# Nine value projections of the first attention quarter, moved ahead of their periods

## The chip, the core and the metric

The kernel runs on one core of a Trainium2 chip, as one program. The time is the device time of one execution in microseconds, the median of several runs. The engines are TensorE (PE, with its weight loads as PEld), VectorE (DVE), ScalarE (ACT) and GpSimd (POOL); SyncE (SP) issues nearly all DMAs of the part that is looked at here.

## What is computed

Two transformer layers, each an attention and a mixture of experts with residuals, on 16 batches of 128 tokens with 512 channels. Only layer 0's attention is touched. It has a self-attention and a cross-attention to a context, 16 query heads and 8 key/value heads each, and one projection over the outputs of both. Cut to what matters, the cross-attention does this:

```python
q  = layernorm_per_head(fp8_linear(ln(x), wqx))        # 16 heads of 128
k  = layernorm_per_head(ctx @ w_kv_x[:1024].T)         # 8 heads
v  = ctx @ w_kv_x[1024:].T                             # 8 heads, only a projection
p  = softmax(q @ k.T / sqrt(128))
out_x = p @ v                                          # then quantized and projected
x  = x + fp8_linear(concat(out_self, out_x), wproj)
```

The value of a batch depends on the context and on the value weights alone, on nothing of x. The matrix products are in float32 or, where one side is exact in fewer bits, in a weight split in two parts.

## The kernel before

Class `Layer0` works through four quarters (`QUARTERS`): cross-attention heads 0 to 7, cross-attention heads 8 to 15, then the two halves of the self-attention. In each quarter it goes over the 16 batches. Batch b of quarter q has the number n = 16q + b. The change touches quarter 0, batches 0 to 9.

The work on a batch is cut into named steps, and these are software-pipelined by hand. `ORDER` is a list of (step, lag): in period p, each step in the list is emitted in turn for batch n = p - lag. All engines follow this order strictly (`InOrder` keeps the program order), so an instruction that waits holds up everything behind it on its engine. SP also issues its DMAs in the order in which they are emitted.

The steps that matter here, with their lag:

- `ln1` to `lnn2` (0): two layernorms of x on DVE, with the power on POOL. `trX` (1): PE transposes the result. `lnT` (1): ACT scales it. `zmul`, `zclip`, `zmsk`, `zadd`, `zsub` (1): POOL, DVE, POOL, DVE bring it onto the quantization grid; the result is `xq`, the queries' input.
- `Kp`, `sqK`, `rsK`, `kn`, `trK`, `kT` (1, kT 2): key projection (PE), squares (ACT), rsqrt (POOL), scaling (DVE), transpose (PE), affine (ACT).
- `Vp`, `v` (3): value projection (PE) and its copy to the tile `v` (ACT); `load_v` fetches its input `xv` from `ctxT` one period earlier. The tag `v` has 3 buffers, `xv` has 2, and the PSUM tag `mm` has 3 banks.
- `Qp0`, `sqQ0`, `rsQ0`, `qn0`, `trQ0`, `qT0`, `sc0`, `nm0`, `exp0`, `pn0`, `trP0`, `pT0`, `pv0` and the same with 1: two chunks of four heads, from query projection to the product with `v` (`pv` uses it at lag 4).
- `po0`, `po1`, `xr`: the output projection and the residual.
- Steps beginning with `W` prepare weights ahead: DVE takes means and cuts a weight into a high and a low part, POOL centres and subtracts, ACT scales, casts and sums the low part.

Before the periods, `start` does the first batch's steps by hand and begins the first weights: the key weights (two pieces of 512 KB), four pieces of query weights (256 KB each), then `xv` and the two pieces of value weights. On PE, the order in the opening is: transpose of x, `Kp`, `Vp`, `trK`, `Qp0`.

In the profile, most instructions have line 69, that of the helper that records them; they are told apart by tile names. `mm<-w,xv` is a value projection, `mm<-w,xk` a key projection, `tr<-ident,xn` is `trX`.

Of the kernel before, what the change touches and what calls it, by code (L numbers as in the profile page):

```python
# [11 lines left out]
F32 = mybir.dt.float32  # L12
# [11 lines left out]
P = 128  # L24
NB = 16
D = 512
# [56 lines left out]
class Ops:  # L83
# [34 lines left out]
    def t(self, pool, shape, dt, tag, bufs=None):  # L118
        self.uid += 1
        return pool.tile(shape, dt, name=f"{tag}_{self.uid}", tag=tag, bufs=bufs)  # L120
# [252 lines left out]

PIECE_STEPS = "lsmckhua"


# [31 lines left out]
def flat(a):  # L410
    return a.rearrange("p c t -> p (c t)")
# [6 lines left out]
class Layer0:  # L418
# [12 lines left out]
    def __init__(self, ops, tc, args, x_dram, vec, router, small, wpool, work, dram, banks, kept_pool, ahead):  # L431
        self.plain, self.tc = ops.nc, tc
        self.kept_pool, self.ahead = kept_pool, ahead
        ops.nc = Engines(tc, ops.nc)
        nc, t = ops.nc, ops.t
        self.ops, self.args, self.x_dram, self.vec, self.router = ops, args, x_dram, vec, router
        self.wpool, self.work, self.banks = wpool, work, banks

        self.kept = {
            kind: [t(dram, [P, D], F32, f"kept_{kind}{b}") for b in range(NB)]  # L440
            for kind in ("lnT", *KINDS)
        }
        self.rin = t(small, [P, 16], F32, "rin")
        nc.vector.reciprocal(self.rin, vec[:, V_INS : V_INS + 16])
        self.rsm = t(small, [P, 32], F32, "rsm")
        nc.vector.reciprocal(self.rsm, vec[:, V_SMOOTH : V_SMOOTH + 32])

        self.ws2 = t(small, [P, 4], F32, "ws2")
        nc.vector.scalar_tensor_tensor(
            self.ws2, vec[:, S_WQ : S_WQ + 4], 1.0 / P, vec[:, S_WQ : S_WQ + 4], ALU.mult, ALU.mult  # L450
        )
        self.pscale = t(small, [P, 1], F32, "pscale")
        nc.vector.tensor_tensor(
            self.pscale, vec[:, S_PROJ_W : S_PROJ_W + 1], vec[:, S_PROJ_IN : S_PROJ_IN + 1],
            ALU.mult,
        )

        self.lw = t(small, [P, 8], F32, "lw")
        for i, (col, scale, by) in enumerate((
            (QLN_W, S_WQ, SCALE), (QLN_B, None, SCALE), (KLN_W, S_WK, 1.0), (KLN_B, None, 1.0),  # L460
            (QXLN_W, S_WQX, SCALE), (QXLN_B, None, SCALE), (KXLN_W, None, 1.0),
            (KXLN_B, None, 1.0),
        )):
            s = 1.0 if scale is None else vec[:, scale : scale + 1]
            nc.vector.tensor_scalar(
                self.lw[:, i : i + 1], vec[:, col : col + 1], s, by, ALU.mult, ALU.mult
            )


        self.w = {}  # L470
        self.units = {"w": W_UNITS, **KEPT_UNITS}
        self.todo = [(q, what) for q in range(4) for what in WEIGHTS]
        self.pieces = [p for q, what in self.todo for p in self.pieces_of(q, what)]
        self.begun, self.finished, self.slots, self.low_steps = [], set(), {}, []
        self.dram, self.made, self.freed, self.period, self.at_step = dram, {}, [], 0, 0
        self.raws = [p for p in self.pieces if p[0] == 0 or p[1] != "v" or self.is_pair(*p[:2])]
        self.pieces = [p for p in self.pieces if p[0]]

        self.low, self.any_low, self.adds = {}, {}, {}
        self.at = [{} for _ in range(4 * NB)]  # L480
# [156 lines left out]

        return added

    def begin(self, centre=None):  # L640
        piece = self.raws.pop(0)
        self.begun.append((piece, self.prepare(*piece, centre)))
        self.advance(self.begun[-1], "l")

    def advance(self, job, until):

        piece, steps = job
        while steps and PIECE_STEPS.index(steps[0][0]) <= PIECE_STEPS.index(until):
            steps.pop(0)[1]()
# [157 lines left out]
    def load_v(self, n):  # L807
        ops, t, s = self.ops, self.ops.t, self.at[n]
        quarter, b = divmod(n, NB)
        if QUARTERS[quarter][0] == 1:  # L810
            s["xv"] = t(self.work, [P, NC, P], F32, "xv", 2)
            ops.nc.sync.dma_start(out=s["xv"], in_=self.args["ctxT"][b])
        else:
            s["xv"] = t(self.work, [P, NC, P], F32R, "xv", 2)
            self.fetch("v", b, s["xv"])
# [6 lines left out]

    def fetch(self, kind, b, out):
        self.ops.nc.sync.dma_start(out=flat(out).bitcast(F32), in_=self.kept[kind][b])

    def step(self, name, n):

        ops, nc, t, work = self.ops, self.ops.nc, self.ops.t, self.work  # L830
        if name[0] != "W":
            quarter, b = divmod(n, NB)
            half = QUARTERS[quarter][0]
            s = self.at[n]
        if name[0] == "W":
            self.piece_step(name, n)
            return
        if name in STEP_NAMES:
            if quarter == 3:
                if name == "rn1":  # L840
                    s["job"] = Routing(self.router, b, s["xr"], work, self.banks)
                getattr(s["job"], STEP_NAMES[name])()
            return
        if name[:2] == "ln" or name == "trX":
            if quarter == 0:
                self.norm_step(name, b, s)
            return
        if name[0] in "zw":
            i = "zw".index(name[0])
            if i < len(MADE[quarter]):  # L850
                self.made_step(name[1:], MADE[quarter][i], b, s)
            return
        c = name[-1]
        if c in "01":
            self.chunk_step(name[:-1], int(c), n, s)
        elif name == "Kp":
            s["k_ps"] = self.project(n, s["xk"], "k")
        elif name == "sqK":
            s["k_ss"] = self.squares(s["k_ps"])
        elif name == "rsK":  # L860
            s["k_rs"] = self.head_rsqrt(
                s["k_ss"], self.ws2[:, 1:2] if half == 0 else 1.0 / P
            )
        elif name == "kn":
            s["kn"] = self.head_scale(s["k_ps"], s["k_rs"], "kn")
        elif name == "trK":
            s["k_tr"] = ops.transpose4(self.banks, s["kn"])
        elif name == "kT":
            s["kT"] = self.affine(s["k_tr"], 2 if half == 0 else 6, "kT", 3)
        elif name == "Vp":  # L870
            s["v_ps"] = self.project(n, s["xv"], "v")
        elif name == "v":
            s["v"] = t(work, [P, D], F32, "v", 3)
            if half == 0:
                nc.scalar.activation(
                    s["v"], s["v_ps"], AF.Copy, scale=self.vec[:, S_WV : S_WV + 1]
                )
            else:
                nc.scalar.copy(s["v"], s["v_ps"])
        elif name == "xr":  # L880
            x = s["xr"]
            nc.vector.scalar_tensor_tensor(x, s["po"], self.pscale, x, ALU.mult, ALU.add)
            nc.sync.dma_start(out=self.x_dram[b], in_=x)
# [135 lines left out]
    def start(self):  # L1019

        nc = self.ops.nc
        self.load(0)
        for what in ("k", "q0"):
            for _ in self.pieces_of(0, what):
                self.begin(nc.vector if what == "q0" else None)
        keys, queries = self.begun[:2], self.begun[2:]
        self.load_v(0)
        for _ in self.pieces_of(0, "v"):
            self.begin()
        for name in ("ln1", "lnp1", "lnn1", "ln2", "lnp2", "lnn2", "trX", "lnT"):  # L1030
            self.step(name, 0)
        self.advance(keys[0], "c")
        for name in ("zmul", "zclip"):
            self.step(name, 0)
        self.advance(keys[1], "c")
        for job in queries:
            self.advance(job, "s")
        for name in ("zmsk", "zadd", "zsub", "Kp", "sqK"):
            self.step(name, 0)
        for job in queries[:2]:  # L1040
            self.advance(job, "u")
        for name in ("rsK", "Vp", "v", "kn", "trK", "kT"):
            self.step(name, 0)
        for job in queries[2:]:
            self.advance(job, "u")

# [6 lines left out]
    def run(self):  # L1053
# [4 lines left out]
        for period in range(4 * NB + lags["xr"]):  # L1058
            self.period = period
            for call, lag in (  # L1060
                (self.load, 0), (self.load_v, lags["Vp"] - 1), (self.load_x, lags["xr"] - 1),
            ):
                n = period - lag
# [4 lines left out]
            for at, (name, lag) in enumerate(ORDER):  # L1068
                if at % 4 == 0:
                    while self.freed and self.freed[0][0] <= period * len(ORDER) + at:  # L1070
                        _, tag, n = self.freed.pop(0)
                        self.units[tag] += n
                    self.refill()
                self.at_step = period * len(ORDER) + at
                if name[0] == "W":
                    lag -= lags["Wl" + name[2]] - 1
                n = period - lag
# [923 lines left out]
```

## Time and profile before

| | |
|---|---|
| median of 3 runs | 3702.06 us (3697.73 to 3706.18) |
| the profiled execution | 3698.0 us, span 3696.2 us |
| mean granted PE clock | 0.982 |
| PE busy | 3532.1 us (96% of the span) |
| DVE, ACT, POOL busy | 1756.6, 1500.5, 1265.6 us |
| quarter 0, to the end of period 12 | the first 264.9 us |
| DMA queue of SP | 338.49 MB, 27.3% of 16 engines' span |

Busy times overlap, since the engines work side by side. An engine can be less busy than PE over the whole span and still set the pace of a stage, so the profile is read by stretches. A timeline line gives the start, the time from the first to the last instruction of a merged group, the engine, the operation, the tiles and the shape; the bracket at its end is the idle time of the engine before it, and what ended that.

### The profile page before, as it was taken

The numbers are of one execution on the slowest core, as the hardware profiler recorded it, in microseconds if no ns is written. First come the engines' busy times: TensorE is split into PE (matmuls) and PEld (weight loads), VectorE is DVE, ScalarE is ACT, GpSimd is POOL, SyncE is SP. The second block draws the span as 40 slices with busy tenths as digits, with TensorE's granted clock in tenths as the row PEclk, the third lists the DMA queues.
The fourth block names the chain that finished last, engine by engine and source line by source line (L and its number), as shares of the span: only waits on it lengthen the run. The fifth ranks groups of instructions, "written<-read, shape, count | busy, mean of one in ns | idle before, by whom it ended". The sixth has DMA issues, their size and how long they took to land. (4 is left out here: it accounts for less than half of the span.)

```text
span 3696.2 us, 42676 instructions
## 1 busy us (share of the span) xinstructions
PE 3532.1 (96%) x13220; PEld 2111.1 (57%) x13220; DVE 1756.6 (48%) x4203; ACT 1500.5 (41%) x5601; POOL 1265.6 (34%) x1596
## 2 busy tenths in 40 slices
PE   6899999999999699999999999899999999997998
PEld 3666666788888444444444454455555555554655
DVE  6888899877688521100000000445555555553111
ACT  5777677788877111101100101443444343441111
POOL 6566677654244222101110100423333333321332
PEclk8999999999999799999999999999999999998999
DMA  4556755744523133453332331000001010006333
GB/s 159 167 175 205 260 199 194 275 147 145 177 90 122 52 115 98 135 167 100 105 91 63 104 76 25 31 23 30 27 22 35 22 32 19 21 12 236 69 63 55
DMA packets 156777, 382.80 MB, mean 104 GB/s; under 512 B 18080, under 2 KB 21312, under 8 KB 154752
## 3 DMA queue, kind: packets, MB, share of 16 engines
q1 hardware_dynamic: 138848, 338.49, 27.3%
q0 software_dynamic: 17696, 41.43, 5.9%
q8 instruction: 119, 1.95, 0.2%
q14 instruction: 114, 0.93, 0.1%
HBM read 266.32 MB, written 113.52 MB: 103 GB/s over the span
## 5 line engine op out<-in xcount | busy, mean ns | idle before, releaser
L69 PE MATMUL h<-xT,w 128*128 128x512 f32 x1024 | 467.2, 594 | 4.0 <-PEq L1322 1.1
L69 PE MATMUL o<-w,hT 128*128 128x512 f32 x1024 | 460.8, 592 | 0.0
L69 ACT ACTIVATE hT<-h 128x512 f32<-128x512 f32 x128 | 76.3, 596 | 852.8 <-PE h L69 852.8
L69 PEld LDWEIGHTS o<-w,hT 128*128 128x128 f32 x1024 | 194.2, 190 | 243.7 <-issue 243.0
L69 DVE COPY xT<-tr 128x512 f32<-128x512 f32 x79 | 54.4, 688 | 572.4 <-PE tr L69 572.4
L69 PEld LDWEIGHTS h<-xT,w 128*128 128x128 f32 x1024 | 189.6, 190 | 231.0 <-issue 229.3
L69 ACT ACTIVATE p<-sc,sm_nm 128x128 f32<-128x128 f32 (+1 forms) x768 | 302.7, 420 | 20.9 <-PE tr L69 10.4
L69 PE MATMUL mm<-w,xq 128*128 128x512 f32 x1024 | 275.8, 411 | 5.5 <-DVE xq L69 4.0
L69 PE MATMUL sc<-kT,qT 128*128 128x128 f32 (+1 forms) x1536 | 267.4, 310 | 4.7 <-ACT qT L69 4.4
L69 ACT ACTIVATE hn_sq<-mm 128x128 f32<-128x128 f32 x768 | 214.8, 280 | 128.1 <-PE mm L69 105.4
L69 POOL DMA_INDIRECT x_dram<-y,e_target x40 | 62.6, 1564 | 572.0 <-ACT y L69 562.3
L69 PE MATMUL pv<-pT,v 128*128 128x256 f32 (+1 forms) x768 | 255.8, 456 | 1.4 <-ACT pT L69 1.4
L69 PEld LDWEIGHTS sc<-kT,qT 128*128 128x128 f32 x1536 | 222.4, 191 | 46.0 <-issue 29.7
L69 PE MATMUL mm<-c_wq,hT 128*128 128x512 f32 x512 | 231.4, 595 | 0.7 <-DVE qn L69 0.7
L69 PE MATMUL po<-c_wo,oT 128*128 128x512 f32 x512 | 231.4, 595 | 0.0
L69 DVE TENSOR_REDUCE sm_nm<-sc 128x4 f32<-128x512 f32 (+1 forms) x256 | 175.5, 685 | 92.1 <-PE sc L69 92.0
L69 PE MATMUL po<-w,cq 128*128 128x512 f32 x512 | 192.4, 457 | 24.8 <-DVE cq L69 3.4
L69 POOL TENSOR_TENSOR hn_rs<-hn_rs,mhalf 128x4 f32<-128x4 f32 x192 | 205.2, 1069 | 16.0
L69 PEld LDWEIGHTS mm<-w,xq 128*128 128x128 f32 x1024 | 185.4, 191 | 43.6 <-DVE xq L69 4.8
L69 ACT ACTIVATE rms_sq<-mm 128x128 f32<-128x128 f32 x384 | 106.8, 278 | 251.5 <-PE mm L69 230.8
L69 PE MATMUL h<-e_w,xT 128*128 (+1 forms) x624 | 200.5, 465 | 4.3 <-DMA e_w<-in_f_w 3.5
L69 PE MATMUL mm<-w,xk 128*128 128x512 f32 x512 | 187.3, 508 | 0.9 <-POOL w L69 0.8
(248 smaller groups left out, 6388.6 us busy)
## 6 DMA issues: line engine op xcount, KB each, us to landing
w<-in_f_w SPq DMA_DIRECT2D x128, 512.0 KB, 3.7
kept_w<-st SPq DMA_DIRECT2D x66, 512.0 KB, 2.9
w<-kept_w SPq DMA_DIRECT2D x66, 512.0 KB, 5.6
x_dram<-xr SPq DMA_DIRECT2D x64, 256.0 KB, 2.0
xr<-x_dram SPq DMA_DIRECT2D x64, 256.0 KB, 2.8
e_w<-in_f_w SPq DMA_DIRECT2D x8, 1408.0 KB
xk<-in_ctxT SPq DMA_DIRECT2D x32, 256.0 KB, 3.8
xv<-in_ctxT SPq DMA_DIRECT2D x32, 256.0 KB, 3.0
```

Source lines behind the costliest of these rows:

```text
L69: return self.tc.keep_in_program_order(call(*args, **kwargs))
```

## The change

The value weights are the first weights to be loaded, ahead of the key weights. Value projections of batches 1 to 9 are made early: four in the opening (`VALUES_FIRST`), and five at named places of periods 2 and 3 (`VALUES_AT`). Each is copied by ACT to a `v` tile and stored in DRAM. In their own periods, `load_v` fetches the stored value in place of the context, and the steps `Vp` and `v` do nothing. Batch 0's value is projected first of all. The order on PE in the opening becomes: `Vp` of batch 0, value 1, transpose of x, value 2, `Kp`, value 3, value 4, `trK`, `Qp0`, value 5. In periods 2 and 3, a value is emitted ahead of the step that `VALUES_AT` names, and its copy and store five steps later (`later`).

```diff
+VALUES_FIRST = 4
+VALUES_AT = ((2, "trX"), (2, "sc0"), (3, "trX"), (3, "trP0"), (3, "trQ1"))
...
     def load_v(self, n):
         ops, t, s = self.ops, self.ops.t, self.at[n]
         quarter, b = divmod(n, NB)
+        if n in self.values:
+            s["v"] = t(self.work, [P, D], F32, "v", 3)
+            ops.nc.sync.dma_start(out=s["v"], in_=self.values[n])
+            return
...
+    def load_value(self):
+
+        n = len(self.values) + 1
+        self.load_v(n)
+        self.values[n] = self.ops.t(self.dram, [P, D], F32, f"value{n}")
+
+    def value(self):
+
+        n = max(self.values)
+        ps = self.project(n, self.at[n]["xv"], "v")
+        if n < VALUES_FIRST + len(VALUES_AT):
+            self.load_value()
+
+        def keep():
+            v = self.ops.t(self.work, [P, D], F32, "v", 3)
+            self.ops.nc.scalar.copy(v, ps)
+            self.ops.nc.sync.dma_start(out=self.values[n], in_=v)
+
+        return keep
...
+        elif n in self.values and name in ("Vp", "v"):
+            pass
...
         self.load(0)
+        for _ in self.pieces_of(0, "v"):
+            self.begin(what="v")
+        self.load_v(0)
+        self.load_value()
         for what in ("k", "q0"):
             for _ in self.pieces_of(0, what):
                 self.begin(nc.vector if what == "q0" else None)
         keys, queries = self.begun[:2], self.begun[2:]
-        self.load_v(0)
-        for _ in self.pieces_of(0, "v"):
-            self.begin()
-        for name in ("ln1", "lnp1", "lnn1", "ln2", "lnp2", "lnn2", "trX", "lnT"):
+        for name in ("Vp", "v"):
+            self.step(name, 0)
+        for name in ("ln1", "lnp1", "lnn1", "ln2", "lnp2", "lnn2"):
+            self.step(name, 0)
+        keep = self.value()
+        for name in ("trX", "lnT"):
             self.step(name, 0)
         self.advance(keys[0], "c")
         for name in ("zmul", "zclip"):
             self.step(name, 0)
+        keep()
+        keep = self.value()
         self.advance(keys[1], "c")
         for job in queries:
             self.advance(job, "s")
-        for name in ("zmsk", "zadd", "zsub", "Kp", "sqK"):
+        for name in ("zmsk", "zadd", "zsub"):
+            self.step(name, 0)
+        keep()
+        for name in ("Kp", "sqK"):
             self.step(name, 0)
         for job in queries[:2]:
             self.advance(job, "u")
-        for name in ("rsK", "Vp", "v", "kn", "trK", "kT"):
+        keep = self.value()
+        for name in ("rsK", "kn"):
             self.step(name, 0)
+        keep()
+        keep = self.value()
+        for name in ("trK", "kT"):
+            self.step(name, 0)
+        keep()
         for job in queries[2:]:
             self.advance(job, "u")
...
                 self.at_step = period * len(ORDER) + at
+                if self.later and self.later[0][0] <= self.at_step:
+                    self.later.pop(0)[1]()
+                if (period, name) in VALUES_AT:
+                    self.later.append((self.at_step + 5, self.value()))
```

More of the change, by code (lines that the diff above doesn't have):

```diff
@@ L473, in __init__ @@
         self.pieces = [p for q, what in self.todo for p in self.pieces_of(q, what)]
+        self.values, self.later = {}, []
         self.begun, self.finished, self.slots, self.low_steps = [], set(), {}, []
@@ L638, in find_low, with begin @@
         return added
-    def begin(self, centre=None):
-        piece = self.raws.pop(0)
+    def begin(self, centre=None, what=None):
+        piece = next(p for p in self.raws if what in (None, p[1]))
+        self.raws.remove(piece)
         self.begun.append((piece, self.prepare(*piece, centre)))
```

## The prediction

> **What bounds the kernel now.** I read the page first:
>
> ```profile
> PE 3532.1 (96%) x13220; PEld 2111.1 (57%) x13220; DVE 1756.6 (48%) x4203; ACT 1500.5 (41%) x5601; POOL 1265.6 (34%) x1596
> ```
>
> TensorE (PE) bounds the whole, but the change touches 265 us of it. So second I cut that stretch at PE's transposes of a batch's input (step trX of batch n opens period n+1; the cuts are its starts on PE's timeline). Columns: length, then busy time of PE, PEld, DVE, ACT, POOL, granted clock, DMA.
>
> ```profile
> 0.00:38.51 38.51, 16.48 (x32) 7.29 (x32) 25.43 (x61) 13.64 (x34) 18.93 (x36) 0.87 0.69 237
> 38.51:57.29 18.78, 11.81 (x36) 7.06 (x37) 12.22 (x25) 8.01 (x31) 13.43 (x15) 0.81 0.35 99
> 57.29:74.74 17.45, 14.06 (x64) 10.45 (x65) 10.11 (x21) 12.21 (x48) 12.23 (x14) 0.90 0.30 91
> 74.74:94.45 19.71, 18.58 (x89) 12.85 (x87) 13.45 (x33) 17.52 (x68) 12.59 (x14) 1.00 0.36 108
> 94.45:124.07 29.62, 21.59 (x92) 14.97 (x91) 17.02 (x37) 19.18 (x72) 13.94 (x16) 0.88 0.41 133
> 124.07:206.63 82.56, 77.45 (x355) 53.01 (x353) 77.44 (x149) 62.99 (x242) 52.85 (x61) 1.00 0.55 185
> 206.63:226.06 19.43, 19.13 (x89) 13.27 (x90) 18.07 (x38) 13.74 (x58) 11.84 (x14) 1.00 0.47 162
> 226.06:245.46 19.40, 19.10 (x91) 13.22 (x90) 17.28 (x37) 14.94 (x62) 11.23 (x13) 1.00 0.53 180
> 245.46:264.87 19.41, 19.11 (x91) 13.23 (x90) 15.32 (x34) 15.48 (x64) 11.21 (x13) 1.00 0.52 177
> ```
>
> The lines are the opening with period 1, then periods 2, 3, 4, 5, 6 to 9, 10, 11, 12. PE has room in the first three. But from period 6 to 10 VectorE (DVE) is as full as PE: it also prepares later weights there. Third, the waits of 144.82 to 226.06, DVE's and PE's:
>
> ```profile
> DVE xn L69 <- POOL ln_rs L69: 2.7, 4, 0.7
> PE tr L69 <- DVE xn L69: 3.6, 4, 1.0
> ```
>
> In four periods DVE waits only 0.7 us each, on its own layernorm chain; PE waits for DVE. There DVE sets the 20.6 us, not PE. Fourth, PE's timeline of the start:
>
> ```profile
> 10.67 1.12 PE L69 MATMUL tr<-ident,xn 128*128 128x128 f32 x4 [10.67 <-DVE xn L69]
> 12.59 6.81 PE L69 MATMUL mm<-w,xk 128*128 128x512 f32 x8 [0.80 <-POOL w L69]
> 19.23 3.60 PE L69 MATMUL mm<-w,xv 128*128 128x512 f32 x8
> 27.68 1.12 PE L69 MATMUL tr<-ident,kn 128*128 128x128 f32 x4 [4.85 <-DVE kn L69]
> 38.51 1.11 PE L69 MATMUL tr<-ident,xn 128*128 128x128 f32 x4 [4.30 <-DVE xn L69]
> 39.42 5.04 PE L69 MATMUL mm<-w,xk 128*128 128x512 f32 x8
> 46.79 1.16 PE L69 MATMUL sc<-kT,qT 128*128 128x128 f32 x8 [1.89 <-ACT qT L69]
> 52.32 3.60 PE L69 MATMUL mm<-w,xq 128*128 128x512 f32 x8 [3.43 <-DVE xq L69]
> 57.29 0.63 PE L69 MATMUL tr<-ident,xn 128*128 128x128 f32 x4 [1.37 <-DVE sm_rs L69]
> 68.27 0.66 PE L69 MATMUL tr<-ident,qn 128*128 128x128 f32 x4 [3.28 <-DVE qn L69]
> ```
>
> PE's gaps here are latencies of a chain that runs through DVE, GpSimd (POOL) and ScalarE (ACT). Fifth, SP's waits from 8 to 12 us:
>
> ```profile
> SPq L693 <- DMA w<-in_wkvx: 1.4, 1, 1.4
> SPq L693 <- DMA raw<-in_wqx: 0.3, 1, 0.3
> ```
>
> SP issues again at 10.30, when the second 512 KB weight piece has landed, and at 10.9, when the 256 KB transfer behind it has: at the start transfers land in order of issue, at nearly 400 GB/s.
>
> **What moves.** A value projection is eight matmul records, 3.43 us from start to the next work (81.36 to 84.79). Nine of them, 30.9 us, leave periods 4 to 12. Four go into the opening, one each before trX and sc0 of period 2, three into period 3 (before trX, trP0, trQ1). The nine ACT copies (0.59) move along. Nine 256 KB stores are new; loading a kept value replaces loading ctxT. The built program has the same number of PE instructions and 18 more on SP.
>
> **Term 1, the opening.** PE runs in program order, and now two value projections (batches 0 and 1) stand ahead of the first transpose. They need both value pieces and xv. These take the places in SP's order that the key pieces and the first q piece had, and so the landing times: second piece 10.3, xv 10.9. PE starts at 11.0. Its price at the start: the first transposes took 1.12 against 0.60 later, so a cold projection costs 3.43 x 1.87 = 6.4; a warm one 3.4. I take 6.0 for the first, near the cold row since it follows 11 us of idleness, and 3.4 for the second. trX starts at 11.0 + 9.4 = 20.4 instead of 10.67: 9.7 later. Everything behind it on three queues waits: lnT (ACT), q_y and q_c (POOL), q_m and xq (DVE, 18.9), and behind xq on DVE the preparation of the first q weights. About 0.9 comes back: the transposes run at full clock (0.5), and q_y no longer waits for the key weights' centring (0.3). The shift is **+8.8**; with a warm first projection +6.4, with the 6.81 that Kp took at the start +9.6. The key weights land at 14.2 instead of 10.3, which then costs nothing: their centring ends near 16, before lnT. Without that cover it would be 3.9. Values 2 to 4 and Kp lie between trX and trK, where PE had 17 us with 10.4 of matmuls partly at half speed. Value 2's xv waits on SP until value 0 is done (about 17) and should land just in time; a miss costs up to 1.
>
> The Trainium skill, "TensorE: Matmul & The Clock Gate", Part 1 (the HAM clock gate), says that PE gets its full clock after about 3.4 us of sustained work. By that rule four of the eight first passes would be cold, the first projection would cost 5.1 (an estimate), and the total would be 0.9 lower; no run here shows it yet.
>
> **Term 2, periods 1 and 2.** Value 5 fits the 4.30 gap before trX. Value 6 stands in the 1.89 gap before sc0, value 7 behind the wait for xq. The denser PE should keep the clock up: Kp of batch 1 took 5.04 instead of 3.60 there, and its 1.4 comes back in the chain to kn and xq. Worked through, trX of period 3 is **+0.3**; bounds 0 and one whole projection, 3.4.
>
> **Term 3, period 3.** Value 8 comes before trP0 and Qp1, where PE has no gap: +3.43 on Qp1, whose squares, rsqrt and scaling then take the same 4.3 us to trQ1. Value 9 fills that gap. ACT's copy of value 8 stands ahead of the squares of Kp, so these, qT and sc0 come some 0.9 late. **+4.3**; bounds 3.4 and 6.9 (both whole).
>
> The copies use the three v buffers, one of which holds batch 0 until period 4, and one batch 1's from period 3. So the copy of value 8 waits for value 7's store, which stands on SP behind two projection weight loads (now issued at 54.23 and 60.71). With the shift it should land about 1 us before value 8 is done: nothing; without that cover ACT stops up to 6.5 us.
>
> **Term 4, what periods 4 to 12 give back.** In period 4 trP1 follows Qp1 at once, but then waits for the softmax on DVE (82.6 to 83.3), and the low-part sum for ACT (87.1): 0.5 of 3.4. In period 5 DVE's wait for sc (1.0) goes: 1.0. The 7 us stall on the last low part is untouched, since it is made by DVE, POOL and ACT. Periods 6 to 10 give 0: DVE is next at once, and PE's 1.0 wait grows to 4.4. In period 11 DVE idles 0.9 beyond its layernorm: 0.9. In period 12 it idles 2.9 in three waits (1.07, 0.93, 0.86), of which I take 2.0, as the ACT and POOL steps in them stay. **-4.4**; bounds -1.5 (5 and 11 half) and -10.6 (3.4 + 3.4 + 0 + 0.9 + 2.9).
>
> **Sum**: 8.8 + 0.3 + 4.3 - 4.4 = +9.0. On the profiled execution (3698.0, span 3696.2) that makes 3707.0; the median is 4.1 above it, 3702.06, so **3711** for the median, 0.24% slower. Nothing after period 12 changes: all of it is tied to periods, not to time. All bounds together reach from -0.8 to +18.4.
>
> **Rivals.** (1) Faster: periods 4 to 12 follow PE after all. All nine projections come back, 30.9 - 13.4 = 17.5: 3685. For it: PE at 96%, 19.3 busy of 20.6 in periods 6 to 9. Against: DVE's 0.7 of waiting. It decides from 20.8 us given back (13.4 + 7.4), six projections; five of the nine are in periods where DVE is full. (2) No change that can be told (0.2%, or 7.4 us, is about what a measurement of this kernel can tell): the first projection is warm, and periods 4, 5 and 12 return 7 together: 6.4 + 0.3 + 4.3 - 7.9 = +3.1, 3705. For it: the granted clock changes often here, and those periods do wait for PE in places (low_sum 2.2 and 2.8). (3) Slower still: ACT stops on the v buffers, +6.5 on the sum: 3718. Against it: SP is mostly idle there.
>
> **Chances.** Forecast 0.52, rival 1 0.08, rival 2 0.32, rival 3 0.08. So faster 0.08, same 0.32, slower 0.60. The range 3703 to 3718 takes in the forecast, rival 2 and rival 3, and leaves out the faster case and the ends of the bounds.
>
> **What would show it.** After: first trX on PE near 20 us; xq of batch 0 near 28; trX of period 3 near 66, of period 4 near 88; periods 6 to 10 still 19.4 to 20.6 long, with PE waiting for DVE some 3.4 us more in each; period 12 near 17.4. The forecast is wrong if trX comes before 15 us, or if periods 6 to 10 shrink to 18 or less.

## The result, and the profile after

The changed kernel takes 3710.11 us in the median (3708.22 to 3715.68, 12 runs), beside 3701.68 us for the kernel before (3697.73 to 3706.18, 12 runs) in the same comparison: a ratio of 1.0024, 95% interval 1.0017 to 1.0032. It is slower by 8.4 us; 3711 was forecast. The profiled execution took 3709.0 us, its span 3707.3 us (before 3698.0 and 3696.2). The page's first part hardly moves:

```profile
PE 3534.7 (95%) x13220; PEld 2110.2 (57%) x13220; DVE 1756.0 (47%) x4203; ACT 1501.8 (41%) x5601; POOL 1269.4 (34%) x1596
```

The work is the same and lies elsewhere, so only a table by stage tells anything. This is the view by stretches of the changed kernel, cut at the same places as before (the starts of trX on PE's timeline). Columns: length, then busy time of PE, PEld, DVE, ACT, POOL, granted clock, DMA.

```profile
0.00:47.97 47.97, 32.12 (x72) 14.26 (x73) 25.61 (x61) 15.68 (x38) 19.60 (x37) 0.96 0.71 234
47.97:66.82 18.85, 16.18 (x53) 9.43 (x52) 12.09 (x25) 9.33 (x34) 14.34 (x16) 0.91 0.52 169
66.82:87.11 20.29, 19.63 (x82) 12.02 (x81) 8.56 (x19) 13.51 (x49) 10.58 (x13) 1.00 0.48 155
87.11:107.87 20.76, 17.04 (x80) 12.54 (x79) 15.08 (x36) 17.15 (x68) 12.58 (x14) 0.92 0.36 115
107.87:136.40 28.53, 19.09 (x84) 13.91 (x83) 15.02 (x34) 19.27 (x71) 12.88 (x16) 0.82 0.44 139
136.40:219.51 83.11, 66.19 (x321) 46.62 (x321) 77.90 (x149) 61.05 (x236) 52.63 (x61) 1.00 0.56 183
219.51:239.05 19.54, 17.35 (x80) 12.63 (x81) 18.17 (x39) 13.24 (x57) 11.85 (x14) 0.91 0.49 162
239.05:256.94 17.89, 16.33 (x82) 11.59 (x81) 15.73 (x34) 14.55 (x61) 12.55 (x13) 1.00 0.52 174
256.94:275.02 18.08, 16.31 (x83) 11.58 (x81) 16.00 (x34) 15.10 (x63) 11.37 (x13) 1.00 0.51 176
```

Lengths against before: opening with period 1 +9.5, period 2 +0.1, period 3 +2.8, period 4 +1.1, period 5 -1.1, periods 6 to 9 +0.6, 10 +0.1, 11 -1.5, 12 -1.3. In periods 6 to 9 PE is 11.3 us less busy than before and the stretch is not shorter, because DVE's 77.4 to 77.9 us fill it. The waits of the changed kernel in periods 7 to 10 (157.66 to 239.05; total, times, longest) say so directly: of DVE's waits the view has only those for its own layernorm chain, and PE waits for DVE.

```profile
DVE xn L69 <- POOL ln_rs L69: 2.7, 4, 0.7
...
PE tr L69 <- DVE p L69: 7.5, 4, 1.9
PE tr L69 <- DVE xn L69: 4.4, 4, 1.1
PE mm L69 <- DVE xq L69: 2.4, 3, 0.8
```

PE's timeline of the opening shows the first loss: the transpose of x starts at 20.16 instead of 10.67, behind two projections that took 9.23 us from their start to that of the transpose.

```profile
10.93 9.40 PE L69 MATMUL mm<-w,xv 128*128 128x512 f32 x16 [10.93 <-DMA xv<-in_ctxT]
20.16 0.60 PE L69 MATMUL tr<-ident,xn 128*128 128x128 f32 x4
20.60 3.60 PE L69 MATMUL mm<-w,xv 128*128 128x512 f32 x8
...
36.45 0.66 PE L69 MATMUL tr<-ident,kn 128*128 128x128 f32 x4 [1.95 <-DVE kn L69]
...
47.97 0.60 PE L69 MATMUL tr<-ident,xn 128*128 128x128 f32 x4
```

On DVE's timeline the chain behind it arrives as late: xq of batch 0 at 27.67 instead of 18.91, and only then can DVE start on the query weights.

```profile
27.67 0.69 DVE L69 TENSOR_TENSOR xq<-q_c,q_m 128x512 fp32r<-128x512 f32 x1 [1.33 <-POOL q_c L69]
```

### The profile page after: what moved, and what is told of

Its sections match the earlier page's. It is cut to its first block, busy times and chain, and to the rows that moved or that the text cites. A ratio compares the mean times of both kernels' runs of the same rounds, so it can differ in the third digit from the quotient of the medians.

```text
span 3707.3 us, 42706 instructions
## 1 busy us (share of the span) xinstructions
PE 3534.7 (95%) x13220; PEld 2110.2 (57%) x13220; DVE 1756.0 (47%) x4203; ACT 1501.8 (41%) x5601; POOL 1269.4 (34%) x1596
## 5 line engine op out<-in xcount | busy, mean ns | idle before, releaser
L69 PE MATMUL mm<-w,xv 128*128 128x512 f32 x512 | 183.4, 502 | 10.9 <-DMA xv<-in_ctxT 10.9
```

The lines of the kernel that those rows point to most:

```text
L69: return self.tc.keep_in_program_order(call(*args, **kwargs))
```

## The experiments

Nine edits were run, and three kernels again for a second profile. This table gives the times, with the ratio to the kernel before of the same comparison:

| kernel | median us | ratio, 95% interval |
|---|---|---|
| changed kernel | 3710.11 | 1.0024 [1.0017, 1.0032] |
| e1 values left out | 3697.05 | 0.9986 [0.9977, 0.9995] |
| e2 turn first | 3706.26 | 1.0014 [1.0005, 1.0023] |
| e3 weights first | 3701.25 | 1.0003 [0.9994, 1.0012] |
| e4 four late values | 3695.81 | 0.9985 [0.9976, 0.9994] |
| e5 five values | 3694.11 | 0.9980 [0.9971, 0.9989] |
| e6 work only | 3698.56 | 0.9989 [0.9979, 0.9998] |
| e7 opening only | 3713.14 | 1.0025 [1.0016, 1.0034] |
| e9 two twice | 3710.83 | 1.0024 [1.0014, 1.0033] |
| e10 batch 14 for 11 | 3694.64 | 0.9982 [0.9973, 0.9991] |

Second profiles (single runs): before 3696.57, changed 3708.38, e1 3699.80. The next table gives the lengths of the stretches in us, all cut at trX on PE's timeline ("op" is the opening with period 1):

| kernel | op | 2 | 3 | 4 | 5 | 6 to 9 | 10 | 11 | 12 | 13 |
|---|---|---|---|---|---|---|---|---|---|---|
| before | 38.51 | 18.78 | 17.45 | 19.71 | 29.62 | 82.56 | 19.43 | 19.40 | 19.41 | 19.65 |
| before, again | 38.16 | 18.40 | 17.32 | 19.69 | 29.50 | 82.52 | 19.44 | 19.41 | 19.41 | 19.62 |
| changed | 47.97 | 18.85 | 20.29 | 20.76 | 28.53 | 83.11 | 19.54 | 17.89 | 18.08 | 19.40 |
| changed, again | 48.17 | 18.87 | 20.29 | 20.87 | 28.64 | 83.07 | 19.35 | 18.07 | 18.06 | 19.41 |
| e1 | 38.29 | 19.37 | 21.21 | 19.00 | 28.84 | 83.08 | 19.56 | 17.87 | 18.08 | 19.58 |
| e1, again | 38.37 | 19.69 | 18.72 | 19.27 | 28.44 | 83.04 | 19.69 | 17.72 | 18.09 | 19.58 |
| e2 | 43.18 | 17.37 | 20.29 | 22.77 | 29.02 | 83.12 | 19.35 | 18.09 | 18.08 | 19.41 |
| e3 | 40.29 | 19.40 | 18.51 | 19.70 | 29.39 | 82.57 | 19.44 | 19.40 | 19.43 | 19.65 |
| e4 | 39.74 | 16.89 | 15.91 | 19.74 | 30.45 | 82.55 | 19.45 | 17.97 | 18.08 | 18.08 |
| e5 | 38.76 | 16.90 | 15.92 | 19.73 | 30.38 | 82.55 | 19.44 | 18.00 | 18.09 | 18.11 |
| e6 | 39.28 | 16.89 | 15.92 | 19.71 | 30.22 | 82.61 | 19.44 | 19.40 | 19.41 | 19.40 |
| e7 | 47.53 | 19.90 | 18.87 | 21.12 | 28.96 | 83.11 | 19.44 | 19.42 | 19.40 | 19.40 |
| e9 | 47.81 | 19.56 | 18.63 | 19.72 | 29.41 | 82.58 | 19.44 | 19.44 | 19.39 | 19.42 |
| e10 | 39.65 | 16.88 | 15.90 | 19.72 | 30.51 | 82.58 | 19.44 | 18.02 | 18.10 | 18.08 |

How far such numbers can be trusted: what follows the start of period 16 took 3371.0 to 3376.7 us in these fourteen profiles, and also differs between two profiles of one kernel (3372.5 and 3375.5 in e1). So a single span says nothing about 3 us; the stretches tell where, the medians how much.

**e1: what the periods give back.** In `load_v` and `step` of the kernel before:

```diff
+LEFT_OUT = range(1, 10)
...
+        if n in LEFT_OUT:
+            s["v"] = t(self.work, [P, D], F32, "v", 3)
+            ops.nc.sync.dma_start(out=s["v"], in_=self.args["x"][b * P : (b + 1) * P, :])
+            return
...
+        elif n in LEFT_OUT and name in ("Vp", "v"):
+            pass
```

> The kernel before, with the value projections of batches 1 to 9 and their copies left out and not made anywhere else; a 256 KB load (rows of x in place of the values) stands where the changed kernel loads a kept value. So it shows only what the periods give back. My theory (DVE sets the pace of periods 6 to 10, the chain through DVE that of most others): about 4.4 us are given back, bounds 1.5 to 10.6, so about 0.9988 of the time before, 3697; periods 6 to 9 together stay within 1 us of 82.6, with PE waiting some 3.4 us more for DVE in each; period 12 near 17.4. Rival (the periods follow PE): all 30.9 us come back, 0.992, 3671; periods 6 to 10 fall to about 17.

Measured: 0.9986, 3697.05 us. Periods 4 to 13 together take 3.8 us less than before (3.8 again between the second profiles), and 6 to 9 take 83.1 (83.0). Periods 4 and 5 alone give back 1.5 in both, which is what the prediction's term 4 had for them. The rival, that the periods follow PE, is out: 30.9 us of work were gone altogether, and an eighth of it came back. Its period 3 took 21.21 us, though nothing is left out there; a second profile was taken for that:

> The kernel with the values of batches 1 to 9 left out, unchanged, for a second profile: its first one had period 3 at 21.21 us and a clock of 0.70, though nothing is left out of the periods before 4, and its median time (3697.05) was 5 us under before while that profile's span was 1.2 us above. My theory: the clock in period 3 is a matter of the single execution; period 3 takes 17.3 to 18.6 this time, period 4 starts at 73 to 76, and the span is 3692 to 3695. Rival (it follows from the kernel): period 3 takes 21.0 to 21.4 again, the span is 3696 to 3699.

Measured: period 3 took 18.72 us, 0.1 above the range given, with the same instructions that took 21.21 in the first profile; so 2.5 us of it did not come from the kernel, but from the single execution or its chip (the two ran on different ones). Period 4 started at 76.78, also past the range, and the span did not fall (3698.1), since the rest behind period 16 was 3 us longer this time.

**e2: the transpose of x ahead of the first values.**

```diff
-        for name in ("Vp", "v"):
-            self.step(name, 0)
-        for name in ("ln1", "lnp1", "lnn1", "ln2", "lnp2", "lnn2"):
+        for name in ("ln1", "lnp1", "lnn1", "ln2", "lnp2", "lnn2", "trX", "lnT", "Vp", "v"):
             self.step(name, 0)
         keep = self.value()
-        for name in ("trX", "lnT"):
-            self.step(name, 0)
```

> The changed kernel, with the transpose and scaling of batch 0's layernorm (trX, lnT) ahead of the first two value projections; loads and all else as in the changed kernel. My theory: the opening is late because the chain from trX to xq and on to the query weights' preparation on DVE stands behind two projections on PE. Then trX is back near 11, xq of batch 0 near 21 to 22 (27.67 changed, 18.91 before; the key weights still land late), the transpose that opens period 2 comes at 42 to 44.5 instead of 47.97, and the time falls by 3.5 to 6 us: 3704 to 3706.5. Rival (the order of the loads, or the mere work of four more projections in the opening, makes it late): no change, the transpose near 48, 3710.

Measured: xq at 21.17, the transpose that opens period 2 as follows on PE's timeline, 4.8 us earlier than in the changed kernel; the median 3706.26, 3.9 less. (Period 4 lost 2.0 of it again, at a granted clock of 0.78.)

```profile
43.18 0.66 PE L69 MATMUL tr<-ident,xn 128*128 128x128 f32 x4 [0.77 <-DVE xn L69]
```

So half of the opening's loss was the order on PE. The other half, 4.7 us, stayed. The late loads are in it (xq is still 2.3 late, and by e3 they cost 1.8 alone); that the rest is the added work of the opening is likely, but no run shows it singly.

**e3: only the loads' order**, on the kernel before.

```diff
...
         self.load(0)
+        for _ in self.pieces_of(0, "v"):
+            self.begin(what="v")
+        self.load_v(0)
         for what in ("k", "q0"):
...
-        self.load_v(0)
-        for _ in self.pieces_of(0, "v"):
-            self.begin()
```

> The kernel before, with only the value weights and the first xv loaded ahead of the key and query weights; no projection is moved. My theory: the means of the key weights start on DVE at 12.9 instead of 10.5 and xq, which stands behind their centring on POOL, is late by the same 2.4; the transpose that opens period 2 near 41 instead of 38.5, the time +2.4 us, 3704. Rivals: the query weights' preparation on DVE waits anyway and hides it, no change (under 1 us, 3702); or the whole 3.9 us of later landing shows, 3706.

Measured: on DVE the first mean of the key weights starts at 12.29 instead of 10.53, xq at 20.68 (before 18.91), and the opening is 1.8 us longer: the means start 1.8 late, not 2.4, and all of that shows; neither rival (nothing, or 3.9) is right. Behind it periods 2 and 3 are 0.6 and 1.1 longer with the same work, at granted clocks of 0.76 and 0.83 instead of 0.81 and 0.90, so that period 4 starts 3.5 us late. The time (1.0003) can't tell it from nothing. In the changed kernel the landing was hidden, as its key means end at 16.9 and the first lnT starts at 20.80; once the transpose goes first, it is not.

**e7: the opening's four values alone.** `VALUES_AT = ()` in the changed kernel.

> The changed kernel with its four early values of the opening alone (batches 1 to 4); batches 5 to 9 are projected in their own periods. My theory: the transpose that opens period 2 comes at 46.5 to 48 (47.97 changed, 38.51 before), and the periods behind it are as before, less 0.5 to 1 in each of periods 4 and 5: period 6 starts 7 to 9 us later than before, at 131 to 133, and periods 6 to 9 last 82.6; 3708 to 3711. Rival (the opening's loss is made up later, and the five values of periods 2 and 3 are what costs): 3702 to 3704.

Measured: 1.0025, the opening at 47.53, period 6 from 136.38, 12.3 us later than before. That is 3.4 us past the range given, and the time 2.1 past its own: nothing came back in period 4, which is longer by 1.4, and periods 2 and 3 are 1.1 and 1.4 longer with no projection of the change in them, at clocks of 0.76 and 0.83. Periods 6 to 9 took 83.1 and not 82.6. The rival, that the opening's loss is made up, is out. Against this kernel the five values of periods 1 to 3 cost little: 0.4, -1.1 and +1.4 us.

**e9: two of those values projected again in their periods**, on e7.

```diff
+TWICE = (1, 2)
...
-        if n in self.values:
+        if n in self.values and n not in TWICE:
...
-        elif n in self.values and name in ("Vp", "v"):
+        elif n in self.values and n not in TWICE and name in ("Vp", "v"):
```

> The changed kernel with its four early values of the opening alone, in which the values of batches 1 and 2 are projected again in their own periods 4 and 5 and the kept ones are not used: 6.9 us more work on PE than in the version with the opening alone, where period 4 took 21.12 us at a granted clock of 0.92 and period 5 28.96. My theory: taking the projection out of period 4 opens a gap of 1.9 us, since the transpose behind it waits for the softmax on DVE, and PE then runs the rest of the period at half rate. With the projection back, period 4 takes 19.6 to 19.9 at a clock of 1.00, period 5 29.4 to 29.8, and the two together are 0.5 to 1 us shorter in spite of the work. Rival (the clock there is an accident of the opening, and PE's work counts): period 4 stays above 21, or takes 21.1 plus a part of 3.4; the two together are 1 to 5 us longer.

Measured: period 4 took 19.72 us instead of 21.12, period 5 29.41 instead of 28.96, period 6 20.77 instead of 21.28: the three are 1.5 us shorter with 6.9 us more work on PE. In all fourteen traces the recorded clock is 1.00 or 0.50 and changes in steps of 3.41 us. Here are such steps in period 4, first of e7 (its period 4 starts at 86.30), then of e9 (from 86.00), then of the second profile of e1 (from 76.78), where the same projection is left out as well; the second column is the length, the third PE's busy time, the third from the end the granted clock:

```profile
94.51:97.92 3.41, 2.25 (x15) 2.03 (x16) 2.41 (x7) 3.32 (x14) 3.07 (x4) 1.00 0.28 77
97.92:101.34 3.42, 2.07 (x9) 1.12 (x9) 2.55 (x7) 2.98 (x13) 1.45 (x3) 1.00 0.45 156
101.34:104.75 3.41, 3.41 (x14) 3.02 (x13) 2.57 (x8) 1.30 (x5) 2.06 (x2) 0.50 0.22 82
```

```profile
94.13:97.54 3.41, 3.41 (x18) 2.21 (x17) 2.46 (x7) 2.98 (x13) 3.07 (x5) 1.00 0.37 87
97.54:100.96 3.42, 2.29 (x9) 1.42 (x9) 2.05 (x6) 3.35 (x12) 1.50 (x2) 1.00 0.66 223
100.96:104.37 3.41, 3.41 (x20) 2.90 (x19) 2.64 (x8) 1.90 (x9) 2.07 (x2) 1.00 0.23 82
```

```profile
84.95:88.36 3.41, 2.23 (x15) 2.02 (x16) 2.42 (x7) 3.31 (x14) 3.08 (x4) 1.00 0.27 77
88.36:91.78 3.42, 2.28 (x11) 1.34 (x11) 2.54 (x7) 2.97 (x13) 1.46 (x2) 1.00 0.44 153
91.78:95.19 3.41, 3.41 (x21) 2.95 (x20) 2.57 (x8) 1.86 (x9) 2.08 (x2) 1.00 0.21 79
```

and, on e7's PE timeline, what stands in the place of the projection that was taken out:

```profile
95.01 0.63 PE L69 MATMUL tr<-ident,p 128*128 128x128 f32 x4 [1.94 <-DVE p L69]
```

Without the projection PE waits 1.94 us for the softmax, then for smaller things, and from 101.34 us its clock is down to 0.50 for one step. With it, the same stretch runs at 1.00. So in e7 the projection was worth more in its place than out of it. The Trainium skill, "TensorE: Matmul & The Clock Gate", section "HAM oscillation — how this bites in real kernels", states as its rule that PE should have no idle gaps above about 3.4 us. By that rule alone the fall would not be expected: the longest gap ahead of it in period 4 was 1.94 us. The measurement decides: several short gaps can be enough.

But the fall does not follow from the removal alone. In e1's second profile PE waits 1.91 us at the same place and then for the same smaller things, the clock stays at 1.00, and period 4 takes 19.27 us (19.00 in the first profile): there the removal gives back 0.4 and 0.7. In all eight profiles with the projection in period 4 it took 19.7 us at 1.00; in the six without it 19.0 to 22.8, with a fall in four. So the rival is right in one thing: what stands ahead of the period counts too.

How it can count is seen in the clock records, though no run varied it alone. From the first clock record of each of the fourteen traces to 350 us, each step at full rate in which PE was busy for less than 43% was followed by one at half rate (36 of 36), none with more than 65% was (of 1129), and 20 of the 99 between were. With the projection no step of period 4 was under 67% (e9). Without it three in a row lay at or in the band between: 58, 66 and 61% in e7, where the clock fell behind the last, and 59, 65 and 67% in e1's second profile, where it did not. So taking the projection out brought the steps into the band where both happen; that their place against the gaps, which shifts with the opening, then decides is likely but not shown.

**e4: four late values, put into waits that exist.** The kernel before with `load_value`, `value` and `later` of the changed one; loads as before; values of batches 8 to 11 only.

```diff
+VALUES = (8, 9, 10, 11)
+VALUES_AT = ((2, "trX"), (2, "Qp0"), (3, "trQ1"))
...
-        for name in ("rsK", "Vp", "v", "kn", "trK", "kT"):
+        for name in ("rsK", "Vp", "v"):
+            self.step(name, 0)
+        keep = self.value()
+        for name in ("kn", "trK"):
             self.step(name, 0)
+        keep()
+        self.step("kT", 0)
```

> The kernel before, loads in its own order, with only the values of batches 8 to 11 made early and kept: one in the opening behind the first value projection, two in period 2 (ahead of trX and of Qp0, where PE waits), one in period 3 (ahead of trQ1, where PE waits). These four leave periods 11 to 14. My theory: the opening shifts by less than 1 us, periods 2 and 3 by at most 2 together, and periods 11 and 12 (with 13 and 14 perhaps) give back 1.5, 1.3 and some 1 to 2 each: 2 to 6 us less than before, 3696 to 3700. Rival (each projection put in early costs its 3.4 us and the later ones give nothing): 3702 to 3710.

Measured: 0.9985, faster than both kernels. Periods 11, 12 and 13 give back 1.4, 1.3 and 1.6, period 14 only 0.2 (19.35 instead of 19.58). Periods 2 and 3 became shorter, by 1.9 and 1.5, which no theory had. In them the clock is 1.00, not 0.81 and 0.90. The opening is 1.2 longer (under 1 was expected) and period 5 0.8.

**e6: the same early work, used for nothing.** e4 without the two branches in `load_v` and `step` that use a kept value.

> The version with four values, whose early projections, copies and stores stay while the periods 11 to 14 project their values again, as before; so PE has 13.7 us more work than before, and nothing is given back. My theory: the early projections lie in PE's waits and keep its clock up, so that they cost nothing: period 11 starts at 224 to 227 (226.06 before), periods 11 and 12 last 19.4 each, the time is 3699 to 3704. Rival (each costs its 3.4 us, or a part, and four values gain only since 13.7 us are taken from the later periods): period 11 starts at 230 to 240, 3706 to 3716.

Measured: period 11 starts at 224.07 (before 226.06 and 225.03), the time is 0.9989. PE has 13.7 us more work, and the kernel is rather faster than slower. Periods 2 and 3 by stretches:

```profile
39.28:56.17 16.89, 11.82 (x45) 6.51 (x44) 11.11 (x24) 10.53 (x36) 13.29 (x15) 1.00 0.53 158
56.17:72.09 15.92, 15.82 (x72) 10.66 (x73) 9.93 (x21) 11.36 (x46) 12.00 (x13) 1.00 0.49 148
```

Three parts in e4's gain can now be told apart: the early work costs nothing, the fuller PE keeps its clock in periods 2 and 3 and gains 1 to 2 us by period 11 (5.75 us by period 16 in e4, 2.25 in e6, against the first profile of before), and periods 11 to 13, each 1.3 to 1.4 shorter than in e6, give back the rest.

**e5 and e10: other batches.** e5 drops batch 11, adds 14 and 15 and puts one projection (its input in a free buffer of the tag xr) into the 6.9 us wait of period 5; e10 is e4 with 14 for 11.

```diff
-VALUES = (8, 9, 10, 11)
+VALUES = (8, 9, 10, 14, 15)    # e5, with (5, "zclip") as a fourth place
+VALUES = (8, 9, 10, 14)        # e10
```

> The version with four values (batches 8 to 11) with batch 11 dropped, since period 14 gave back only 0.2 us, and batches 14 and 15 added: in their periods 17 and 18 PE is never idle before and DVE is busy 17.1 and 15.9 of 20 us. The fifth projection stands in period 5, where PE waits 6.9 us for the last low part. My theory: the projection in that wait is free and keeps PE's clock up behind it (start of period 6 is 1 to 2 us earlier against the start of period 5 than with four values, where it took 30.45); periods 17 and 18 give back about 1.4 each; 2 to 5 us less than with four values, 3691 to 3694. Rival (its copy delays the low part's chain on ACT, and other engines hold periods 17 and 18): no gain over four values, 3695 to 3698.

> The version with four values, with batch 14 in the place of batch 11. In the version with five, period 17 (batch 14) took 17.26 us from one key projection to the next instead of 18.98, and period 18 (batch 15) 22.16 instead of 18.99, with PE waiting 3.9 us for DVE, which waited 4.5 us for a store. My theory: batch 14 gives 1.7 where batch 11 gave 0.2, and period 18 stays near 19 with its projection in place: 1 to 1.5 us less than with four values, 3694 to 3695, which the times can hardly tell; the trace does. Rival (the store decides period 18 whatever PE does): period 18 takes 20.5 to 22 and the gain is given back, 3696.

Measured: 0.9980 and 0.9982, which these intervals can't tell from e4's 0.9985. In the traces, e5's projection in the wait of period 5 was free but did not save the clock (period 5 30.38; a wait of 3.49 us is left behind it). From one key projection to the next, period 17 took 17.26 and 17.22 instead of 18.98, as expected. Period 18 did not: 22.16 without its projection (before 18.99), 19.63 with it. The rival's 20.5 to 22 for e10 is out, but 0.6 of the 1.8 was given back there. In e10 period 19 then took 21.74 instead of 20.17; since it took 20.03 to 21.97 in the twelve profiles with unchanged work there, that says nothing. In e5, DVE's longest wait in period 18 is for a store, and PE waits for DVE; here DVE's wait (total, times, longest), then PE's timeline:

```profile
DVE z L69 <- DMA kept_v<-z: 4.9, 2, 4.5
```

```profile
366.32 1.09 PE L69 MATMUL tr<-ident,p 128*128 128x128 f32 x4 [3.87 <-DVE p L69]
```

**Second profiles of before and of the changed kernel.**

> The kernel before, unchanged, for a second profile of it. In the profile of the kernel with the values left out, period 3 took 21.21 us at a granted clock of 0.70 and in the first profile of before 17.45 at 0.90, with the same work in it. My theory: the granted clock of the sparse periods 2, 3 and 5 differs between executions, and their lengths with it by up to 4 us, while periods 6 to 12 repeat within 0.2. Rival (the clock follows from the order of the work): all periods repeat within 0.3.

> The changed kernel, unchanged, for a second profile. My theory: the opening, period 3 (clock 1.00) and periods 6 to 13 repeat within 0.4 us; periods 2, 4 and 5, whose granted clock was 0.91, 0.92 and 0.82, may differ by up to 2 us. Rival (these too follow from the order of the work alone): all repeat within 0.3.

Measured: both repeat, the changed kernel within 0.2 us in every stretch, the kernel before within 0.4. My theory, that the clock of the sparse periods differs between executions of these two, is not borne out; of the three kernels profiled twice, only e1's period 3 differed by microseconds (granted clock 0.70 and 0.83). But the same work of period 3 took 17.3 to 21.2 us over before, e1, e3, e7 and e9. The steps of the clock record (under e9) would explain both, if a small shift tips one of them; no run tried that.

## Why the prediction was right, point by point

**Term 1, the opening (+8.8): right, by its own steps.** PE's start was 10.93 (11.0), the two projections took 9.2 (9.4), trX came at 20.16 (20.4), xq 8.8 late (8.8 predicted for everything behind trX). With value 5 before it, trX of batch 1 is 9.5 and 10.0 late in the two pairs of profiles; +9.1 was the sum of terms 1 and 2 up to period 3, where 9.5 to 10.5 were measured. e2 shows the mechanism for half of the loss: with trX first, 4.8 of 9.5 us are back. The cover that the text named for the late key weights is real, but without it they cost 1.8 (e3), not the 3.9 given. The first projection took 9.23 to the start of trX less 3.4 for the second, 5.8; 6.0 was taken. Two small sums are off: 0.5 and 0.3 make 0.8 where 0.9 is written, and a warm first projection makes +6.2, not +6.4; neither moves the forecast by more than 0.1. The estimate from the Trainium skill's page "TensorE: Matmul & The Clock Gate", Part 1, 5.1, was 0.7 short.

**Term 2, periods 1 and 2 (+0.3): right.** Period 2 is +0.1 and +0.5 long, with its clock up from 0.81 to 0.91.

**Term 3, period 3 (+4.3): right in its direction, 1.4 too large**: 2.84 and 2.97 measured. Up to trQ1 the working holds: it comes 15.4 us into the period instead of 11.0, 4.4 later. What the term left out is the clock behind it: the query projection there took 3.66 us before (at 69.47) and 2.13 in the changed kernel (at 83.39), so 1.5 came back. The buffers held: ACT has no wait for a v buffer in the first 120 us, so rival 3 did not occur.

**Term 4, the give-back (-4.4): period 4 was wrong.** Period 5 gave 1.1 and 0.9, as said (1.0), but period 4 became 1.1 and 1.2 longer instead of 0.5 shorter, so that the two together gave nothing (49.29 and 49.51, before 49.33 and 49.19): the step failed at "0.5 of 3.4". It subtracted a projection from a wait and left the clock as it was. In e1, where the clock stayed, period 4 did give back 0.7 and 0.4; in the changed kernel, as in e7 beside e9, the emptier PE runs part of the period at half rate. Periods 6 to 10, "DVE is next at once", gave nothing, as said; they lost 0.6 in place of 0, nearly all of it in period 6 (21.26, before 20.75) and only where the values of periods 4 and 5 were missing (e1, e2 and e7 have it, e9 not); why was not tried. Periods 11 and 12 gave 1.5 and 1.3 (0.9 and 2.0 said), the sum right, and period 13 0.2.

**The sum.** +9.0 said, +9.9 and +11.3 found up to period 16 in the two pairs of profiles, +8.4 in the medians. Term 3 was too high by 1.4, term 4 too generous by 2.2 and term 1 too low by 0.7. These cancel in part, to +10.2 at the end of period 12; that the sum was better than its parts is luck.

**Rivals.** (1) is refuted by e1: with all nine projections left out, 3.8 us come back and not 30.9. (2) and (3) did not happen: the first projection was cold, periods 4, 5 and 12 returned 1.4 together and not 7, and ACT was not stopped. The base for (2), that the granted clock moves things here by microseconds, was true; it worked for the change in period 3 and against it in period 4.

## What to carry to other kernels

Moving work off an engine pays only in stretches where that engine sets the pace and nothing is next at once: of the nine periods two gave back 1.3 to 1.5 us of 3.4 each, five nothing because DVE was as full, one (period 5) 1.1, and one (period 4) lost as much, because the clock fell. Put moved work into waits of the receiving engine, behind the start of the longest chain and not ahead of it; choosing four values by the first rule and their places by the second turned 0.24% slower into 0.15% faster. And price a removal with the clock: PE work that seems superfluous may be what keeps PE at full rate.

## What the runs showed of the hardware that was not expected

- More work made PE faster (e6): in periods 2 and 3 one more projection of 3.4 us in each shortened the periods from 18.78 and 17.45 to 16.89 and 15.92, at a granted clock of 1.00 instead of 0.81 and 0.90.
- The clock fell to 0.50 behind gaps of at most 1.94 us (e7, period 4), and stayed at 1.00 behind gaps of at most 1.91 us in the same place (e1, second profile).
- The recorded clock changed in steps of 3.41 us, and in these traces it fell behind every step with PE busy under 43% and behind none over 65% (counted under e9).
- The column of the granted clock shows 1.00 in 10.90 to 13.00 of the changed kernel, while the first two passes there took 2.08 us together and a later one 0.43. That trace's first clock record is at 15.52 us, so at the very start of PE's work the column doesn't show the slow passes; their durations do.
